# Out-projection, query and key/value projections moved between two key tiles of the scores

## The chip, the cores and the metric

The kernel runs on one core of one Trainium2 chip. A core has a matrix engine (TensorE, in the profile PE, its weight loads PEld) that writes to PSUM, and three engines that work on vectors: VectorE (DVE), ScalarE (ACT) and GpSimd (POOL). SyncE (SP) issues DMAs. Each engine works through its own queue in order; semaphores make one engine wait for another. The metric is the device time of one execution in microseconds (us). The kernel before takes 1353.22 us, the median of three runs.

## The reference

An input `x` (2048 x 256) goes through a cross attention over 1601 context rows of width 192 (and one learned key and value ahead of them, so 1602 keys), with 16 heads of width 64, and then through a feed-forward network with weights of +1 and -1.

```python
x1 = layernorm(layernorm_plain(x)) * g_norm
q, k, v = x1 @ Wq, ctx @ Wkv[:, :1024], ctx @ Wkv[:, 1024:]
k, v = [null_k; k], [null_v; v]            # 1602 keys
a = softmax(q k^T / 8, masked)             # per head
x = x + layernorm(concat(a v) @ Wout) * g_out
h = relu(s0 * [xn, -xn] @ k0) * 2;  h = relu(s1 * h @ k1) * 2
x = x + s2 * h @ k2                        # xn = layernorm(x); k0, k1, k2 are signs
```

The softmax needs the maximum of each query's scores before the exponentials, and the sum of the exponentials after them.

## The kernel before

The work is cut into units `(p, b)`: `p` counts eight pairs of heads, `b` four blocks of 512 queries, 32 units in all, `b` running fastest. The two heads of a pair lie in the two halves of the 128 partitions, so that a matmul of head 0 and one of head 1 use the two row halves of TensorE together. Keys are cut into 13 tiles of 128 (the last has 66).

One unit has three stages on PE.

*Scores* (loop over `k`, `exps` at line 284 and `max_chunk` at line 251). For each key tile, `sT` = keys times queries in full fp32 (L296). For tiles 0 and 1 the negated maxima `mT` are added by a small matmul with ones (L307), because key tiles are kept as differences to the tile two before (`keys_stepped`, line 216, on POOL), so that even and odd tiles accumulate in two PSUM buffers that are never restarted. ACT makes the exponential `e` (L309), and POOL adds all `e` up to `acc` (L498, L500). Beside this, in the same loop, PE computes the scores of the *next* unit a first time, with rounded operands, in 16 chunks (L259: four query tiles by four key ranges of 400), and DVE reduces each chunk to its maximum (L262). One chunk goes with each tile, two with tiles 0, 4 and 8 (`extra`). `max_combined` (L267) joins them to `mcol`.

*Values* (`weighted`, line 312): 13 pairs of matmuls accumulate `av`, with the two heads in the two column halves of the array (L316). After the third pair, `divided` (line 331) forms the denominators of the unit before (L334, `den`); DVE takes the reciprocal (L336, 3.36 us) and multiplies (L337) to `aoT`. ACT copies `av` to `avs` (L542).

*Projections*, with the full array: for the next pair of heads `project_v` (L230, copied by ACT at L238, and in the first block a row copied by DVE at L242) and `project_k` (L207; DVE writes `kT` at L211 and the rounded, filled `kr` at L212), spread over the blocks by `ahead`: block 0 takes values 0, 1 and keys 0; block 1 values 2, 3 and keys 1; block 2 keys 2, 3 and the differences on POOL (L221); block 3 nothing. Then `project_out` of the unit before (L324, added to `y_sb` by DVE at L329), `max_turned` (L272: `mcol` transposed by PE, spread by DVE to `mT` at L274), and `project_q` for the unit after the next (L196; ACT writes `qr` at L197 and `qT` at L198).

PSUM is used as two pairs of buffers of two banks each. `spare` holds the two `sT` buffers, then `av`, then some projections; `flex` holds the chunks of the maxima, `den`, the turned maxima and the other projections. A buffer is taken again only when what was in it has been read. The order is written out by hand (`manual_schedule`): each engine's queue has its instructions in the order in which the Python code issues them; only the waits are added. Weights are loaded by SP at the start of a pair's first unit for the pair after it (line 164), and run ahead as buffers come free.

Units 0 and 1 have something of their own: each normalizes one more input block of 512 rows (`input_root`, `input_normed`, on DVE and ACT), turned by PE in the projections (`input_turned`, L361). Units 28 and 29 prepare the first layer's weights `w0` on DVE (L526, L528), unit 30 normalizes the first output block. After the 32 units come the three layers of the feed-forward network.

## Time and profile before

| | us |
|---|---|
| median of 3 runs (1353.21 to 1353.57) | 1353.22 |
| the profiled execution | 1355.55 |
| its span, first to last instruction | 1353.7 |
| PE busy | 1329.3 |
| POOL busy | 994.8 |
| DVE busy | 880.7 |
| ACT busy | 607.7 |
| scores of a unit | 16.5 |
| values of a unit | 12.17 |
| projections, blocks 0, 1, 2, 3 | 8.68, 7.32, 6.44, 3.75 |

The stages are read from the starts of PE's matmuls in the middle of the run; they repeat from pair to pair within 0.1 us, so a pair of heads takes 4 x (16.5 + 12.17) + 26.2 = 141 us. The feed-forward network begins at about 1164 us.

How to read the profile: a group of instructions has its line, engine and operation, then `out<-in` by the program's names with shapes, a count, the busy time and mean length of one, and behind a bar the engine's idle time before them and what ended it. In a timeline, the columns are start, length, engine, line; neighbours of one group are merged (`x5`), and brackets give the idle time before and who ended it. [...] The granted PE clock was 0.992 of full on average.

### The profile page before, as it was taken

The page shows a single profiled execution, that of the slowest core. Times are in us where ns is not written, and L with a number is a line of the kernel's source. Part 1 is how long each engine was busy: PE and PEld are TensorE (multiplying, and loading weights), DVE is VectorE, ACT ScalarE, POOL GpSimd, SP SyncE. Part 2 cuts the span into 40 slices and gives each one's busy share as a digit, 9 for nine tenths or more (in the row PEclk, how much of TensorE's full clock was granted, in tenths as well). Part 3 has the DMA queues.
Part 4 walks back from the last instruction along what each step waited for, and adds up shares of the span by engine and source line. Part 5 has one row for each costly group of instructions (what it writes and reads, how often), then busy time and mean ns, then how long its engine had stood idle before and what let it go on. Part 6 is the DMA issues. An engine that isn't in the chain of part 4 may idle for free.

```text
span 1353.7 us, 16255 instructions
## 1 busy us (share of the span) xinstructions
PE 1329.3 (98%) x6528; PEld 664.6 (49%) x6528; DVE 880.7 (65%) x957; ACT 607.7 (45%) x655; POOL 994.8 (73%) x492
## 2 busy tenths in 40 slices
PE   6999999999999999999999999999999999999998
PEld 3544444444444444444444444444444443688887
DVE  5677776676667756686767656767676884464431
ACT  1666454445444454444544454454445557421220
POOL 4377987798888987798779877987798999711100
PEclk9799999999999999999999999999999999999999
DMA  5000000000000000000000000000000010000000
GB/s 136 4 1 7 0 1 8 8 1 0 8 1 7 1 1 8 7 1 1 7 8 1 1 8 8 0 1 5 0 16 1 1 39 0 1 0 16 16 16 16
DMA packets 14940, 12.31 MB, mean 9 GB/s; under 512 B 2240, under 2 KB 14784, under 8 KB 14864
## 3 DMA queue, kind: packets, MB, share of 16 engines
q1 hardware_dynamic: 13552, 9.70, 2.5%
q10 hardware_dynamic: 832, 1.23, 0.3%
q8 instruction: 51, 0.84, 0.3%
q0 software_dynamic: 480, 0.34, 0.1%
q14 instruction: 25, 0.20, 0.1%
HBM read 9.17 MB, written 2.10 MB: 8 GB/s over the span
## 4 chain that ended last, share of the span: by engine, by line
PE 93%; DVE 3%; ACT 2%; DMA 1%; issue 0%; POOL 0%; SPq 0%; ACTq 0%
PE sT L296 28%; PE av L316 27%; PE ps L592 10%; PE max L259 8%; PE psq L196 4%; PE po L324 4%; PE psv L230 3%; PE psk L207 3%; PE ps L615 2%; PE den L334 2%; ACT e L309 1%; PE sT L307 1%; DVE mx L262 1%; DMA x_sb<-in_x 1%; PE xT L361 0%
## 5 line engine op out<-in xcount | busy, mean ns | idle before, releaser
L500 POOL TENSOR_TENSOR acc<-acc,e 128x1024 f32<-128x1024 f32 (+1 forms) x352 | 847.3, 2407 | 27.6
L262 DVE TENSOR_REDUCE mx<-max 128x2 f32<-128x800 f32 (+1 forms) x512 | 481.3, 988 | 70.9 <-PE max L259 61.2
L309 ACT ACTIVATE e<-sT,maskb 128x1024 f32<-128x1024 f32 (+1 forms) x416 | 460.0, 1115 | 64.0 <-PE sT L296 38.0
L296 PE MATMUL sT<-qT,kT 64*128 64x512 f32 (+1 forms) x1664 | 444.4, 612 | 1.6 <-ACT e L309 1.4
L316 PE MATMUL av<-e,v 128*64 128x512 f32 (+1 forms) x1664 | 369.5, 594 | 1.0
L259 PE MATMUL max<-kr,qr 64*128 64x400 f32 (+1 forms) x1024 | 285.7, 568 | 2.3 <-DVE mx L262 1.5
L316 PEld LDWEIGHTS av<-e,v 128*64 128x64 f32 (+1 forms) x1664 | 116.7, 137 | 239.0 <-issue 219.3
L259 PEld LDWEIGHTS max<-kr,qr 64*128 64x128 f32 x1024 | 97.3, 186 | 187.2 <-DVE mx L262 149.7
L296 PEld LDWEIGHTS sT<-qT,kT 64*128 64x128 f32 (+1 forms) x1664 | 135.3, 181 | 104.8 <-ACT e L309 81.5
L498 POOL TENSOR_TENSOR acc<-e,e 128x1024 f32<-128x1024 f32 x32 | 75.5, 2358 | 147.6 <-ACT e L309 147.6
L542 ACT COPY avs<-av 128x512 f32<-128x512 f32 x32 | 18.8, 587 | 327.0 <-PE av L316 327.0
L336 DVE RECIPROCAL aoT<-den 128x512 f32<-128x512 f32 x31 | 104.1, 3357 | 70.0 <-PE den L334 70.0
L197 ACT ACTIVATE qr<-psq 128x512 fp32r<-128x512 f32 x32 | 19.1, 597 | 139.1 <-PE psq L196 139.1
L592 PE MATMUL ps<-h0hi,w 128*128 128x512 f32 x256 | 79.5, 392 | 0.0
L592 PE MATMUL ps<-h0lo,w 128*128 128x512 f32 x256 | 78.9, 389 | 0.0
L211 DVE TENSOR_TENSOR kT<-psk,keep 128x400 f32<-128x400 f32 (+1 forms) x32 | 18.4, 574 | 90.0 <-PE psk L207 89.8
L119 POOL TENSOR_TENSOR y_sb<-y_sb,gout_sb 128x256 f32<-128x256 f32 x12 | 9.3, 776 | 90.1 <-DVE y_sb L86 90.1
L581 DVE SCALAR_TENSOR_TENSOR h1lo<-ps,h1hi 128x1024 fp32r<-128x1024 f32 x16 | 19.6, 1224 | 69.0 <-ACT h1hi L580 69.0
L196 PE MATMUL psq<-xnT,wq 128*128 128x512 f32 x128 | 62.2, 610 | 0.6 <-DVE kT L211 0.6
L324 PE MATMUL po<-wo,aoT 128*128 128x256 f32 x256 | 61.5, 383 | 0.0
L329 DVE TENSOR_TENSOR y_sb<-po,y_sb 128x1024 f32<-128x1024 f32 x28 | 34.2, 1220 | 40.0 <-PE po L324 39.8
L580 ACT ACTIVATE h1hi<-ps 128x1024 fp32r<-128x1024 f32 x16 | 16.4, 1027 | 94.6 <-PE ps L592 94.6
(125 smaller groups left out, 1054.8 us busy)
## 6 DMA issues: line engine op xcount, KB each, us to landing
x_sb<-in_x SPq DMA_DIRECT2D x4, 512.0 KB, 8.7
out_x<-o SPq DMA_DIRECT2D x8, 256.0 KB, 2.1
wkv<-in_wkv SPq DMA_DIRECT2D x16, 96.0 KB, 2.1
wq<-in_wq SPq DMA_DIRECT2D x8, 128.0 KB, 2.3
wo<-in_wout SPq DMA_DIRECT2D x8, 128.0 KB, 2.1
xnT<-in_k SPq DMA_DIRECT2D x1, 1024.0 KB, 5.9
ctx_sb<-in_ctxT ACTq DMA_DIRECT2D x3, 300.0 KB, 7.9
xnT<-in_k SPq DMA_DIRECT2D x1, 512.0 KB, 3.9
```

The source lines that it names most:

```text
L196: nc.tensor.matmul(ps[:, 0, :], weights[p][0][:, c, :], xnT[:, b, c, :], start=c == 0, stop=c == 1)
L207: nc.tensor.matmul(ps[:, 0, :w], weights[p][1][:, c, 0, :], ctx_sb[:, c, keys], start=c == 0, stop=c == 1)
L259: nc.tensor.matmul(ps[:, j, :w], queries[p, b][1][rows, ts(t, 128)], pairs[p][2][rows, ds(start, w)], start=True, stop=True)
L262: nc.vector.tensor_reduce(maxima[p, b][:, t, :, c], ps[:, :, :w], AX.X, ALU.max)
L296: nc.tensor.matmul(ps[:n, j, :], kT[rows, ds(128 * k, n)], qT[rows, :], start=k < 2, stop=k >= 2, skip_group_check=k >= 2,)
L309: nc.scalar.activation(e[:n], ps[:n], AF.Exp, bias=maskb[:n, k : k + 1])
L316: nc.tensor.matmul(av[ts(j, DH), 0, :], v[:n, k, ts(j, DH)], e[:n, j, :], start=k == 0, stop=k == KC - 1)
L324: nc.tensor.matmul(pv[:, t, :], aoT[:, ts(t, 128)], weights[p][2], start=True, stop=True)
L336: nc.vector.reciprocal(aoT, ps)
L498: nc.gpsimd.tensor_tensor(acc, es[0], es[1], ALU.add)
L500: nc.gpsimd.tensor_tensor(acc[:m], acc[:m], es[k][:m], ALU.add)
L592: nc.tensor.matmul(ps[:, f, :], w(c)[:, ts(2 * g + f, 128)], parts[part][:, c, :], start=i == 0, stop=i == len(steps) - 1,)
```

## The change

The three stages become two and an insert. The function `projections(u)` holds what stood after the values; in all units but the first it is called inside the scores loop, ahead of tile 7 (`HALF`), so after tile 6 and its chunk. `project_out` there is that of the unit two back. `max_turned` now follows the values directly, and uses two matmuls against the identity, one for each 64 columns of `mcol`, in place of one transpose over the full array. All projections use `flex`. The doubled chunks go with tiles 0, 7 and 10. Unit 0 normalizes both remaining input blocks and calls `projections(0)` at its end. Buffers: `qT` three, `qr` two, `mx` one; `ones` becomes a view of `ones_r`. The work itself, operation by operation, is otherwise the same.

```diff
-    ones = cp.tile([128, DH], F32, name="ones")
+    ones_r = cp.tile([128, 128], F32R, name="ones_r")
+    ones = ones_r.bitcast(F32)[:, :DH]
...
-            qT = wp.tile([128, 512], F32, tag="qT", name=f"qT_{p}_{b}")
-            qr = wp.tile([128, 512], F32R, tag="qr", name=f"qr_{p}_{b}", bufs=1)
+            qT = wp.tile([128, 512], F32, tag="qT", name=f"qT_{p}_{b}", bufs=3)
+            qr = wp.tile([128, 512], F32R, tag="qr", name=f"qr_{p}_{b}")
...
-            nc.tensor.transpose(ps[:, 0, :128], mcol, ident)
+            for j in range(2):
+                nc.tensor.matmul(ps[ts(j, DH), 0, :128], mcol[:, ts(j, DH)], ident, start=True, stop=True)
...
-            po = spare(f"po_{p}_{b}")
+            po = flex(f"po_{p}_{b}")
...
-        extra = {0, 4, 8}
+        extra = {0, 7, 10}
+        HALF = 7
...
+        def projections(u):
+            nonlocal quotient
+            p, b = units[u]
+            if quotient is not None:
+                project_out(*quotient)
+                quotient = None
+            if u < 2:
+                input_turned(u + 2)
+            if u + 2 < len(units):
+                project_q(*units[u + 2])
+            if p + 1 < NP:
+                for n in ahead[b][0]:
+                    project_v(p + 1, n)
+                for n in ahead[b][1]:
+                    project_k(p + 1, n)
+                if b == 2:
+                    keys_stepped(p + 1)
...
+                    if k == HALF and u > 0:
+                        projections(u)
                     es.append(exps(p, b, k, sT))
...
-                if u < 2:
-                    input_normed(u + 2, *input_root(u + 2), beside=True)
+                if u == 0:
+                    roots = [input_root(c) for c in (2, 3)]
+                    for c in (2, 3):
+                        input_normed(c, *roots[c - 2], beside=True)
                     nc.scalar.activation(warm, eps_sb, AF.Exp)
...
-                    if k == 2 and last is not None:
-                        aoT = divided(*last, flex(f"den_{p}_{b}")[:, 0, :])
+                    if k == 2 and owed is not None:
+                        quotient = (*owed[:2], divided(*owed, flex(f"den_{p}_{b}")[:, 0, :]))
...
                 nc.scalar.copy(avs, av[:, 0, :])
-                if u < 2:
-                    input_turned(u + 2)
-                if p + 1 < NP:
-                    for n in ahead[b][0]:
-                        project_v(p + 1, n, spare if n % 2 else flex)
-                    for n in ahead[b][1]:
-                        project_k(p + 1, n, spare if n % 2 else flex)
-                    if b == 2:
-                        keys_stepped(p + 1)
+                owed = (p, b, avs, acc)
+                if nxt is not None:
+                    max_turned(*nxt)
+                if u == 0:
+                    projections(0)
                 if nxt is None:
                     uT = turned(0)
-                if last is not None:
-                    project_out(*last[:2], aoT)
-                if nxt is not None:
-                    max_turned(*nxt)
-                if u + 2 < len(units):
-                    project_q(*units[u + 2])
-                last = (p, b, avs, acc)
+                    project_out(*quotient)
+        last = owed
```

More of the change, by code (lines that the diff above doesn't have):

```diff
@@ L156, in xattn_ffn @@
         maskb = ap.tile([128, KC], F32, name="maskb")
-        ones_r = ap.tile([128, 128], F32R, name="ones_r")
         mcol = ap.tile([128, 128], F32, name="mcol")
@@ L253, in max_chunk @@
             if n == 0:
-                maxima[p, b] = wp.tile([128, 4, 2, 4], F32, tag="mx", name=f"mx_{p}_{b}")
+                maxima[p, b] = wp.tile([128, 4, 2, 4], F32, tag="mx", name=f"mx_{p}_{b}", bufs=1)
             start, w = CHUNKS[c]
@@ L413, in xattn_ffn @@
         nc.gpsimd.memset(maskb, 0.0)
-        nc.gpsimd.memset(ones, 1.0)
         nc.gpsimd.memset(fan, 1.0)
@@ L460, in xattn_ffn @@
         begin.__exit__(None, None, None)
-        last = None
+        owed = None
+        quotient = None
[4 more added lines that the diff above has]
+                project_out(*quotient)
+                quotient = None
+            if u < 2:
[9 more added lines that the diff above has]
+                    keys_stepped(p + 1)
         with tc.manual_schedule():
```

## The prediction

> **What bounds the kernel now.** I read the page first: engines, then the chain. TensorE (PE) is busy nearly always and the chain is 93% PE, so one must see which part of its time is work and which is waiting with a matmul open.

> ```profile
> span 1353.7 us, 16255 instructions
> PE 1329.3 (98%) x6528; PEld 664.6 (49%) x6528; DVE 880.7 (65%) x957; ACT 607.7 (45%) x655; POOL 994.8 (73%) x492
> PE 93%; DVE 3%; ACT 2%; DMA 1%; issue 0%; POOL 0%; SPq 0%; ACTq 0%
> ```

> Then the busy time by window: scores, attention times values, projections of unit (3,1), then the next scores.

> ```profile
> 511.10:527.59 16.49, 16.45 (x89) 7.18 (x88) 14.14 (x16) 14.44 (x15) 11.96 (x6) 1.00 0.01 4
> 527.59:539.76 12.17, 12.17 (x56) 3.93 (x56) 5.23 (x4) 1.00 (x1) 11.86 (x5) 1.00 0.01 2
> 539.76:547.08 7.32, 7.32 (x39) 5.23 (x37) 3.37 (x4) 1.33 (x3) 4.97 (x3) 1.00 0.00 0
> ```

> Columns: length, then PE, weight loads, DVE, ACT, POOL. In the scores three engines are over 85% busy; afterwards DVE, ACT and, in the projections, POOL have time. The timeline of the next scores shows what paces them.

> ```profile
> 552.44 2.22 ACT L309 ACTIVATE e<-sT,maskb 128x1024 f32<-128x1024 f32 x2 [0.19 <-PE sT L296]
> 555.03 2.21 ACT L309 ACTIVATE e<-sT,maskb 128x1024 f32<-128x1024 f32 x2 [0.37 <-PE sT L296]
> 552.56 4.79 DVE L262 TENSOR_REDUCE mx<-max 128x2 f32<-128x804 f32 x5 [0.20 <-PE max L259]
> 557.54 4.79 DVE L262 TENSOR_REDUCE mx<-max 128x2 f32<-128x800 f32 x5 [0.20 <-PE max L259]
> ```

> Four tiles and five chunks take 4.98 us: five reduces of 4.79 and one gap. PE waits for both engines:

> ```profile
> PEld max L259 <- DVE mx L262: 145.3, 336, 0.7
> PEld sT L296 <- ACT e L309: 71.0, 184, 0.5
> ```

> PE's own streams are shorter. From starts in the timeline: a score tile 0.855 (two passes of 0.43), a shift 0.215, a chunk 0.175. Then 13 x 0.855 + 2 x 0.215 + 16 x 0.175 = 14.35 of 16.5: about 2.1 us per unit is round trips through two-buffer PSUM. Values (14 pairs of 0.86) and projections run dense.

> The last view is DVE's short operations and POOL's in the projections:

> ```profile
> L212 DVE SCALAR_TENSOR_TENSOR kr<-drop,nullk,kT x32: 635/698/2126, 14.4 to 1002.3; 128x400 fp32r<-128x400 uint8 x24, 128x402 fp32r<-128x402 uint8 x8
> 578.87 0.56 DVE L211 TENSOR_TENSOR kT<-psk,keep 128x400 f32<-128x400 f32 x1
> 579.47 2.12 DVE L212 SCALAR_TENSOR_TENSOR kr<-drop,nullk,kT 128x400 fp32r<-128x400 uint8 x1
> ```

> ```profile
> 573.73 7.43 POOL L500 TENSOR_TENSOR acc<-acc,e 128x1024 f32<-128x1024 f32 x3
> 581.67 1.94 POOL L221 TENSOR_TENSOR kT<-kT 128x66 f32<-128x66 f32 x3 [0.51 <-DVE kr L212]
> ```

> `kr` costs 0.64 us, or up to 2.1: the long one at 579.47 ends 0.43 after POOL's addition ends (581.16), and so do the other long ones. Today PE works on and nobody waits.

> [...]`kr`, with two SBUF inputs, waits for POOL's end; the reduces, the eviction of `psk` (0.56 to 0.58) and `mT`, with one operand in PSUM, never vary. [...]from the last stream of `psq` (ends 511.00) to the first of `sT` (511.20) it is 0.2 us. [...]

> **The change, part by part.** Per-unit accounting, T0 = end of the last `av` stream. Latencies from the timeline: a result is there 0.165 after its stream, DVE starts 0.045 later, ACT 0.115; PE's next stream starts 0.16 after an engine's end; reduces follow at 0.90.

> *Mode switches.* Before: rows, columns, full, rows: three. After: rows, full, rows, columns, rows: four. +0.2 per unit. The maxima in halves stay in `av`'s mode: two passes of 128 columns, 0.21 against 0.11, +0.1. Sum +0.3. `mT` (0.68) starts at T0+0.42, done at 1.10; the first tile streams from 0.41 to 1.27, so it hides `mT`.

> *First half, tiles 0 to 6.* The same waits as today: tile 6 streams at 8.0, chunk 7 at 8.86 to 9.04. `po` needs chunk 6's buffer: chunk 6 streams at 7.72, reduced at 9.09; `po` at 9.25, just the mode switch. Nothing gained or lost.

> *Projections.* Streams as before: `po` 1.72, `psq` 1.71, `psv` 1.83 each, `psk` 1.34. All use the two `flex` buffers now, so two waits appear. b=1: `psk` waits until ACT has copied `psv2`: 0.57. b=2: the second `psk` waits for both copies of `psq`: 0.28.

> *Second half, tiles 7 to 12.* It has eight chunks in six tiles, 8 x 0.90 = 7.2 us of DVE against 6 x 0.855 + 8 x 0.175 = 6.5 of PE: it is DVE's pace that sets it. Without obstacles reduce 8 starts 1.4 after the last projection, and chunk 10 streams at +2.57. The end of the last projection to the next `av` is then 7.9. Check on b=3: 9.25 + 3.43 (`po`, `psq`) + 7.9 = 20.6, against 16.5 + 3.75 = 20.25 now: +0.3, just the switch and the halves, and the 2.1 us of round trips stay. ACT's copies of `psq` and `psv` (0.6 each) stand ahead of tile 7's exponential; they are done before tile 7 has streamed, save in b=3, where chunk 9 waits 0.4 for the second copy of `psq`; DVE's slower pace covers that. But reduce 8 is queued on DVE behind the evictions of `psk`, and POOL, which adds from T0+4.4 in steps of 2.43 (ends 14.0, 16.45, 18.9), is now always busy there:
> - b=3: no `psk`. +0.3.
> - b=0: last stream ends 17.68, `kT` until 18.46, `kr` waits for 18.9, ends 19.4, column copy, reduce 8 ends 20.4, chunk 10 at 20.6 instead of 20.25. The row copy (L242) waits for 16.45, ahead of `kT`. 0.3 + 0.3 = +0.6.
> - b=1: ends 16.88, `kT` until 17.66, `kr` 19.3, reduce 8 ends 20.3, chunk 10 at 20.43 instead of 19.45: 1.0. With 0.57 and 0.3, less 0.1 that overlaps: +1.8.
> - b=2: first `kr` at 14.8 ends 16.9; `kT` 17.4; POOL's next, lengthened, ends 19.1, second `kr` 19.5; reduce 8 ends 20.5, chunk 10 at 20.64 instead of 18.21: 2.4. With 0.28 and 0.3, less 0.1: +2.9.

> One pair: 5.6 us. Six ordinary pairs: 33.6. Bounds: [...]with later waits absorbed, 0.3 + 0.8 + 0.5 + 0.3 = 1.9; with POOL half a step off against me, 8.5.

> *Moved and added elsewhere.* POOL's key differences (3.9 us, L221) stand between additions 6 and 7; POOL needs 30 us of 35, its lag ends inside the next unit, nobody waits. SP's loads of weights are issued a pair ahead, `wo` lands 2.1 us after issue: no wait. `project_out` two back reads an `aoT` long finished; if it weren't, `po` would stop PE, but L337 ends at least 2 us before T0, and `po` comes 9 us later. `ones` as a view of `ones_r` takes one POOL memset from the start, off the path.

> *First pair.* Unit 0 normalizes both remaining input blocks before `avs`: ACT at present starts its eight operations at 72.47 and needs 3.9; the second statistics (2.2 on DVE), eight more (3.9) and the table load end at about 83.7, against `av`'s end at 78.9. `avs`, `xnT`, then `psq` wait: +4.6. Unit 1: no `po` yet (-1.7), `psq` waits for `xnT` (+1.2), plus its 1.8: +1.3. Units 2, 3: 3.2. Sum 9.1.

> *Last pair.* 3 x 0.3; `w0` (3.4 and 4.4 us, ends 1100.9 against T0 = 1098.7) now stands ahead of `mT` with no projections to hide it: +0.8 and +2.0; in the last unit `po` costs about 0.8, the rest under the last exponentials. Sum 4.5.

> Total 33.6 + 9.1 + 4.5 = 47 on the profiled span 1353.7 (its execution 1355.55, 1.85 outside the span). The median is 1353.22; the difference is laid on it: 1400.

> **Rivals.** (1) [...]`kr` finds gaps. Then 6 x 1.9 + 7.5 + 4.5 = 23, 1376. For: it takes 0.64 in all b=0 units today; against: there POOL had finished, here it is in mid-chain. (2) Faster: the break lets ACT finish tiles 5 and 6 and DVE two chunks under the projections, so tiles 7 and 8 need not wait, and half of the 2.1 us of round trips goes: 1.0 - 0.3 = 0.7 per unit, 27 units, 19; less the 9 at the two ends: 1343. For: the idle DVE and ACT in the third window; against: only two chunks fit into PSUM, and eight follow in six tiles. It decides if reduce 8 follows its matmul within 0.4 us on average. (3) Moved work without effect: only if gains of rival 2 meet losses of mine. That the program doesn't do as told is excluded: its instruction order shows `po`, `psq`, `psv`, `psk` after chunk 7 and tile 7 after them.

> **How the numbers follow.** Forecast (1375 to 1422) 0.72; rival 1 (1366 to 1380) 0.13; rival 2 0.12; within 0.2%, about what a measurement can tell from no change, 0.03. The range is 1366 to 1420: it leaves out rivals 2 and 3 and a little of the upper bound. Slower 0.85.

> **What would show it.** Right: scores before tile 7 about 9.2 from T0, b=2 longest against before (38 us per unit), `kr` at 1.5 to 2.1 inside the scores and the reduce after it late, a PE gap of over 4 us after unit 0's values. Wrong: `kr` at 0.64, or a second half under 7 us.

## The result and the profile after

The kernel after takes 1401.94 us (median of 4 runs, 1399.09 to 1403.38), the kernel before 1353.22 (1352.55 to 1353.57) on the same chip: 1.0358 times as long, 95% interval 1.034 to 1.0376. The profiled execution took 1401.85 us with a span of 1400.1, 46.4 more than before's 1353.7.

The page of the kernel after, in the lines that answer to those of before (engines' busy time, then the chain by engine):

```profile
span 1400.1 us, 16434 instructions
PE 1339.9 (96%) x6624; PEld 676.1 (48%) x6624; DVE 896.3 (64%) x957; ACT 604.5 (43%) x652; POOL 987.2 (71%) x491
...
PE 81%; DVE 12%; ACT 4%; POOL 1%; issue 1%; DMA 1%; ACTq 0%; SPq 0%; DVEq 0%; POOLq 0%
```

PE's busy time rose by 11, the span by 46: the kernel doesn't work much more, it waits. The chain's share of DVE went from 3% to 12%. That tells the engine; the stages tell the place. Busy time by window in unit (3,2): the turned maxima (`mt`) with the first half of the scores, projections, second half, values; then the second half of unit (3,0). The columns are length, PE, weight loads, DVE, ACT, POOL, granted clock.

```profile
569.90:579.10 9.20, 9.20 (x54) 4.14 (x50) 7.36 (x8) 7.28 (x8) 4.69 (x2) 1.00 0.00 0
579.10:585.55 6.45, 6.45 (x24) 3.64 (x22) 3.52 (x4) 2.19 (x3) 6.21 (x4) 1.00 0.00 0
585.55:595.73 10.18, 7.67 (x41) 3.32 (x41) 10.14 (x10) 5.55 (x6) 9.19 (x9) 1.00 0.00 0
595.73:607.80 12.07, 12.07 (x56) 4.07 (x58) 5.73 (x5) 0.98 (x1) 11.68 (x6) 1.00 0.01 1
...
512.12:520.15 8.03, 7.42 (x41) 3.40 (x40) 7.78 (x10) 5.50 (x5) 6.55 (x4) 1.00 0.01 2
```

Only the third window is bad: of 10.18 us PE has 7.67, DVE is busy in 10.14. DVE's timeline there, with POOL's two lines between:

```profile
584.21 0.57 DVE L211 TENSOR_TENSOR kT<-psk,keep 128x400 f32<-128x400 f32 x1 [1.84 <-PE psk L207]
584.82 2.03 DVE L212 SCALAR_TENSOR_TENSOR kr<-drop,nullk,kT 128x400 fp32r<-128x400 uint8 x1
586.77 0.56 DVE L211 TENSOR_TENSOR kT<-psk,keep 128x400 f32<-128x400 f32 x1
587.37 2.12 DVE L212 SCALAR_TENSOR_TENSOR kr<-drop,nullk,kT 128x400 fp32r<-128x400 uint8 x1
589.41 7.30 DVE L262 TENSOR_REDUCE mx<-max 128x2 f32<-128x804 f32 x8
...
581.63 7.42 POOL L525 TENSOR_TENSOR acc<-acc,e 128x1024 f32<-128x1024 f32 x3
589.57 4.35 POOL L221 TENSOR_TENSOR kT<-kT 128x66 f32<-128x66 f32 x6 [0.52 <-DVE kr L212]
```

POOL's third addition ends at 589.05, the second `kr` at 589.49, 0.44 later; only then does DVE begin the eight reductions, 3.9 us after the second half began. The first of them, that of chunk 8, is called reduction 8 below. Over the whole run the group of `kr` (least, median, longest in ns; the median was 698 before):

```profile
L212 DVE SCALAR_TENSOR_TENSOR kr<-drop,nullk,kT x32: 635/1739/2127, 14.5 to 1027.1; 128x400 fp32r<-128x400 uint8 x24, 128x402 fp32r<-128x402 uint8 x8
```

From the starts of PE's matmuls (in the timeline their lengths overlap: those of `av` are 0.59 us long and start in pairs 0.43 us apart), the stages of every ordinary pair after, against the unit's sum before (in pairs 5 and 6, counted from 0, block 1 has halves of 9.14 and 8.45 with the same sum):

| block | `mt` | first half | projections | second half | values | sum | before | more |
|---|---|---|---|---|---|---|---|---|
| 0 | 0.32 | 8.89 | 8.57 | 8.03 | 12.07 | 37.88 | 37.35 | +0.5 |
| 1 | 0.32 | 8.89 | 7.71 | 8.71 | 12.07 | 37.70 | 35.99 | +1.7 |
| 2 | 0.32 | 8.89 | 6.43 | 10.20 or 11.55 | 12.07 | 37.9 or 39.3 | 35.16 | +2.8 or +4.1 |
| 3 | 0.32 | 8.89 | 3.64 | 7.68 | 12.07 | 32.60 | 32.42 | +0.2 |

The 46.4 us: six ordinary pairs +35.0 (5.83 each), the first pair +12.3, the last with the feed-forward network +2.6, and -3.5 in the opening. The opening's part is hardly the change's: the values of unit 0 end at 75.1 to 79.3 us over the twelve kernels of this study (78.9 in before, 75.4 in after, 76.7 in experiment 4, whose opening is that of after, and 75.1 in before with experiment 8's edit), and PE's granted clock in the first 50 us is 0.80 in before and 0.86 in after (0.90 in the first 51 us of experiment 9).

The first pair's part begins in unit 0. PE and ACT there, in the timeline:

```profile
75.73 1.09 PE L363 MATMUL xT<-ident,y_sb 128*128 128x128 f32 x8
81.67 3.78 PE L196 MATMUL psq<-xnT,wq 128*128 128x512 f32 x4 [4.85 <-ACT xnT L364]
85.24 5.00 PE L230 MATMUL psv<-wkv,ctx_sb 96*128 96x128 f32 x32
...
79.06 1.28 ACT L542 ACT_TABLE_LOAD   x1
80.46 0.57 ACT L569 COPY avs<-av 128x512 f32<-128x512 f32 x1
80.93 0.69 ACT L364 ACTIVATE xnT<-xT,gn_sb 128x512 f32<-128x512 f32 x1
```

PE stands for 4.85 us, and afterwards is slower: 3.78 and 5.00 where experiment 9 below has 1.98 and 3.74. The granted clock is 0.74 from 84.0 to 91.5 us.

### The profile page after: what moved, and what is told of

It reads as the page before. It is cut to its first block, busy times and chain, and to the rows that moved or that the text cites. A ratio compares the mean times of both kernels' runs of the same rounds, so it can differ in the third digit from the quotient of the medians.

```text
span 1400.1 us, 16434 instructions
## 1 busy us (share of the span) xinstructions
PE 1339.9 (96%) x6624; PEld 676.1 (48%) x6624; DVE 896.3 (64%) x957; ACT 604.5 (43%) x652; POOL 987.2 (71%) x491
## 4 chain that ended last, share of the span: by engine, by line
PE 81%; DVE 12%; ACT 4%; POOL 1%; issue 1%; DMA 1%; ACTq 0%; SPq 0%; DVEq 0%; POOLq 0%
PE av L318 25%; PE sT L298 22%; PE ps L609 9%; PE max L259 6%; DVE mx L262 5%; PE po L326 4%; PE psq L196 4%; DVE kr L212 3%; PE psv L230 3%; ACT e L311 2%; PE psk L207 2%; PE ps L632 2%; PE den L336 2%; DVE kT L211 1%; PE sT L309 1%; POOL acc L525 1%
## 5 line engine op out<-in xcount | busy, mean ns | idle before, releaser
L525 POOL TENSOR_TENSOR acc<-acc,e 128x1024 f32<-128x1024 f32 (+1 forms) x352 | 840.3, 2387 | 37.9 <-ACT e L311 11.9
L262 DVE TENSOR_REDUCE mx<-max 128x2 f32<-128x800 f32 (+1 forms) x512 | 480.3, 986 | 72.6 <-PE max L259 63.8
L298 PE MATMUL sT<-qT,kT 64*128 64x512 f32 (+1 forms) x1664 | 451.0, 620 | 1.7 <-ACT e L311 1.4
L259 PE MATMUL max<-kr,qr 64*128 64x400 f32 (+1 forms) x1024 | 288.4, 578 | 31.6 <-DVE mx L262 26.7
L523 POOL TENSOR_TENSOR acc<-e,e 128x1024 f32<-128x1024 f32 x32 | 75.4, 2358 | 191.4 <-ACT e L311 191.4
L259 PEld LDWEIGHTS max<-kr,qr 64*128 64x128 f32 x1024 | 98.2, 188 | 206.6 <-DVE mx L262 152.6
L298 PEld LDWEIGHTS sT<-qT,kT 64*128 64x128 f32 (+1 forms) x1664 | 139.3, 184 | 96.6 <-ACT e L311 66.2
L276 DVE TENSOR_TENSOR mT<-mt,fan 128x512 fp32r<-128x512 f32 x32 | 22.1, 690 | 98.4 <-PE mt L274 98.4
L609 PE MATMUL ps<-h0lo,w 128*128 128x512 f32 x256 | 78.9, 389 | 0.0
L339 DVE TENSOR_TENSOR aoT<-avs,aoT 128x512 f32<-128x512 f32 x32 | 59.6, 1863 | 2.6
L207 PE MATMUL psk<-ctx_sb,wkv 96*128 96x400 f32 (+1 forms) x128 | 51.2, 532 | 7.6 <-DMA ctx_sb<-in_ctxT 4.8
```

Of the source, the lines that this page charges most:

```text
L207: nc.tensor.matmul(ps[:, 0, :w], weights[p][1][:, c, 0, :], ctx_sb[:, c, keys], start=c == 0, stop=c == 1)
L259: nc.tensor.matmul(ps[:, j, :w], queries[p, b][1][rows, ts(t, 128)], pairs[p][2][rows, ds(start, w)], start=True, stop=True)
L262: nc.vector.tensor_reduce(maxima[p, b][:, t, :, c], ps[:, :, :w], AX.X, ALU.max)
L298: nc.tensor.matmul(ps[:n, j, :], kT[rows, ds(128 * k, n)], qT[rows, :], start=k < 2, stop=k >= 2, skip_group_check=k >= 2,)
L523: nc.gpsimd.tensor_tensor(acc, es[0], es[1], ALU.add)
L525: nc.gpsimd.tensor_tensor(acc[:m], acc[:m], es[k][:m], ALU.add)
```

## The experiments

Theory: `kr`, which reads two operands from SBUF, waits for POOL's additions (every long one in the traces of before and after ends 0.43 to 0.44 us after one), and in the new place reduction 8, and so PE, is queued behind it. Rivals: the break with its mode switches costs by itself (A); any work ahead of reduction 8 costs, however short (B); the wait for two flex buffers instead of four (C, D). A fourth question is the first pair. All times are medians beside the kernel before on the same chip (1352.66 for the first four, 1354.95 for the next four, 1354.22 for the last two).

**Experiment 1: `kr` without the second SBUF operand.**

```diff
-nc.vector.scalar_tensor_tensor(kr[:, keys], drop[:, keys], nullk[:, 0:1], kT[:, keys], ALU.mult, ALU.add)
+nc.vector.scalar_tensor_tensor(kr[:, keys], drop[:, keys], nullk[:, 0:1], ps[:, 0, :w], ALU.mult, ALU.add)
```

> The kernel after, but kr (L212) adds drop*nullk to psk in PSUM instead of to kT in SBUF, so that it has one SBUF operand; it leaves out the masking of the keys for the maxima only. Theory ([...]reduce 8 is queued behind it): kr 0.60 to 0.75 us in all 32, second half of the scores in b=2 down from 10.2 or 11.55 to about 8.3, b=1 from 8.7 to about 7.8, b=0 from 8.0 to about 7.8; per pair 3.4 to 4.6 less, 24 to 32 in all: 1370 to 1378, point 1374. Rival A (the break itself, its mode switches, costs the time): 1398 to 1403. Rival B (any work between the projections and reduce 8 costs, however short[...]): kr short but the second halves within 0.3 of those of after, 1392 or more.

1372.1 us (1370.4 to 1374.61), 1.0147 times before (1.0132 to 1.0162): by the ratios about 29 of the 48 us are gone. The group, and DVE in a unit of block 2:

```profile
L212 DVE SCALAR_TENSOR_TENSOR kr<-drop,nullk,psk x32: 617/623/625, 14.7 to 1001.4; 128x400 fp32r<-128x400 uint8 x24, 128x402 fp32r<-128x402 uint8 x8
...
573.38 0.57 DVE L211 TENSOR_TENSOR kT<-psk,keep 128x400 f32<-128x400 f32 x1 [0.33 <-PE psk L207]
573.87 0.62 DVE L212 SCALAR_TENSOR_TENSOR kr<-drop,nullk,psk 128x400 fp32r<-128x400 uint8 x1
574.62 3.69 DVE L262 TENSOR_REDUCE mx<-max 128x2 f32<-128x804 f32 x4
```

The same operation with one operand in PSUM took 617 to 625 ns in all 32, beside the same additions of POOL. All second halves become 7.68 to 8.03; the granted clock, which fell in four of the block 2 units of after, is 0.992 on average here and 0.987 there. The order of the work was not touched, so A, as the main cause, and B for blocks 1 and 2 fall: work of ordinary length stands ahead of reduction 8 at no cost there.

**Experiment 2: key projections first**, so that `kT` and `kr` stand on DVE ahead of `po`, `psq` and `psv`.

```diff
+            if p + 1 < NP:
+                for n in ahead[b][1]:
+                    project_k(p + 1, n)
+                if b == 2:
+                    keys_stepped(p + 1)
             if quotient is not None:
...
-                for n in ahead[b][1]:
-                    project_k(p + 1, n)
-                if b == 2:
-                    keys_stepped(p + 1)
```

> The kernel after, with the key projections (and POOL's key differences) put first among the projections, so that kT and kr stand on DVE a few us ahead of reduce 8; nothing else moves. Theory: kr stays at 1.5 to 2.1 us in b=1 and 2, but the second halves come to 7.6 to 7.9 in all four units; b=2 gets a new wait of 0.5 before its third projection, since the second kT is queued behind the first long kr; b=1 loses the wait of psk for psv2. Per pair 3.3 to 4.8 less: 1367 to 1378, point 1372. Rival A (break and mode switches): 1398 to 1403. Rival C (the wait for flex buffers in the projections is the main part): the projection stages keep their length and the time stays above 1390.

1367.82 us (1367.58 to 1371.75), 1.0123 (1.0106 to 1.014). The second halves are 7.68 to 7.72 in all blocks, the projection stages 8.56, 7.21, 6.33 and 3.64: b=1's wait for `psv2` was 0.50 us, b=2's 0.10. C had the smallest part. One thing came out otherwise: `kr`, now a few us earlier, is mostly short here (median 639 ns). For blocks 0 and 1 this run therefore does not separate place from length. For block 2 it does: the second `kr` is still 1.94 long in every pair, yet the second half is 7.68, and reduction 8 waits for its chunk and not for DVE:

```profile
564.14 1.94 DVE L212 SCALAR_TENSOR_TENSOR kr<-drop,nullk,kT 128x400 fp32r<-128x400 uint8 x1
566.00 1.21 DVE L331 TENSOR_TENSOR y_sb<-po,y_sb 128x1024 f32<-128x1024 f32 x1
568.22 7.52 DVE L262 TENSOR_REDUCE mx<-max 128x2 f32<-128x804 f32 x8 [1.01 <-PE max L259]
```

In two units of block 1 a `kr` of 2.80 did cost time, to what stood behind it in the new place:

```profile
810.15 2.80 DVE L212 SCALAR_TENSOR_TENSOR kr<-drop,nullk,kT 128x400 fp32r<-128x400 uint8 x1
812.88 1.21 DVE L331 TENSOR_TENSOR y_sb<-po,y_sb 128x1024 f32<-128x1024 f32 x1
```

The eviction of `po` came late, its flex buffer with it, and the projections of these two units took 8.67 instead of 7.21.

**Experiment 3: block 3 normalized by DVE**, to free ACT in unit 0.

```diff
-input_normed(c, *roots[c - 2], beside=True)
+input_normed(c, *roots[c - 2], beside=c == 2)
```

> The kernel after, with the normalization of input block 3 in unit 0 done by DVE (four operations, as the opening does for block 0) instead of by ACT's eight; both square roots stay where they are. Theory for the first pair (avs waits in ACT's queue behind sixteen operations and a table load, PE idles 4.85 us and runs slower for a while after): ACT reaches avs before av ends, the gap after unit 0's values is under 1.5 us and psq and psv take their usual 1.7 and 1.8: 5 to 7.5 less, 1394.5 to 1397, point 1395.5. Rival (the gap is the two statistics on DVE or the table load, not the eight operations): under 1.5 us gained, 1400 to 1402.

1403.76 us (1401.39 to 1405.49), 1.0379 (1.0363 to 1.0394): nothing gained, a miss. Here is DVE, then ACT:

```profile
74.90 9.75 DVE L87 TENSOR_SCALAR y_sb<-x_sb,mv_x,rstd_x 128x256 f32<-128x256 f32 x4
...
85.48 0.68 DVE L276 TENSOR_TENSOR mT<-mt,fan 128x512 fp32r<-128x512 f32 x1
...
80.11 0.57 ACT L569 COPY avs<-av 128x512 f32<-128x512 f32 x1
80.57 0.69 ACT L364 ACTIVATE xnT<-xT,gn_sb 128x512 f32<-128x512 f32 x1
```

Each of the four operations took about 2.45 us, one step of POOL's additions (2.43), and `mT` and DVE's half of `xnT` stood behind them. They have one tensor from SBUF, where `kr` has two. The same operation from 1236 us on in after took up to 0.90 us instead of 0.41 when it met an operation of POOL, and ended 0.15 after it. So the edit moved the work into another wait for POOL, and says nothing of ACT's part.

**Experiment 4: the block of projections between the last tile and the values** instead of between tiles 6 and 7.

```diff
-                    if k == HALF and u > 0:
-                        projections(u)
...
+                if u > 0:
+                    projections(u)
                 if nxt is not None:
                     max_combined(*nxt)
```

> The kernel after, with the block of projections put between the last score tile and the values instead of between tiles 6 and 7 (unit 0 as in after). Maxima in halves, buffers and the order within the block are unchanged; what is no longer there is the break inside the scores, one mode switch, and DVE's reductions queued behind kT and kr. Theory: seven pairs lose nearly all of their 5.8 extra, but for the halves (0.1 per unit), up to 0.85 per pair of flex waits, and a short wait of po for the reduction of chunk 14; first pair's unit 0 still costs its 7.5: 1360 to 1372, point 1365. Rival A (the mode switches): 0.2 per unit less than after, about 1395. Rival D (the two flex buffers instead of four are the cost): above 1385.

1377.18 us (1376.79 to 1377.55), 1.0183 (1.0168 to 1.0198): 25 less than after by the medians, 24 by the ratios, and 5 more than the upper end expected. A and D, as expectations of 1395 and above 1385, fall. It is also the cleanest look at a long `kr` that costs nothing, in a unit of block 2:

```profile
580.37 1.44 DVE L212 SCALAR_TENSOR_TENSOR kr<-drop,nullk,kT 128x400 fp32r<-128x400 uint8 x1
581.74 0.56 DVE L211 TENSOR_TENSOR kT<-psk,keep 128x400 f32<-128x400 f32 x1
582.33 2.13 DVE L212 SCALAR_TENSOR_TENSOR kr<-drop,nullk,kT 128x400 fp32r<-128x400 uint8 x1
...
581.09 2.79 PE L318 MATMUL av<-e,v 128*64 128x512 f32 x12
```

`av` runs on beside them. This is before's situation. What remains is 0.42 to 0.47 per unit (0.93 in b=1, with the wait for `psv2`): 0.21 for `mt`, and 0.31 at the end of the scores, where `po` waits for the reduction of chunk 14 and its flex buffer, while before `av` goes on in `spare`.

**Experiment 5: normalization in one ACT operation** (scale and bias together), eight operations instead of sixteen in unit 0. A flag, not shown below, keeps the old form for the other callers.

```diff
-nc.vector.tensor_scalar(nm, mv[:, :, 0], -1.0, None, ALU.mult)
+nc.vector.scalar_tensor_tensor(nm, mv[:, :, 0], -1.0, r, ALU.mult, ALU.mult)
...
-nc.scalar.activation(dst[:, t, :], src[:, t, :], AF.Identity, bias=nm[:, j : j + 1])
-nc.scalar.mul(dst[:, t, :], dst[:, t, :], r[:, j : j + 1])
+nc.scalar.activation(dst[:, t, :], src[:, t, :], AF.Identity, bias=nm[:, j : j + 1], scale=r[:, j : j + 1])
```

> The kernel after, with the normalization of input blocks 2 and 3 in unit 0 in one ACT operation per 128 rows (scale 1/std, bias -mean/std) instead of two: ACT does 8 operations of 0.5 us there instead of 16; DVE does no more than in after. Theory for the first pair (avs and xnT wait in ACT's queue behind the sixteen operations and the table load): ACT is free about 4 us earlier, at the end of av; PE's gap after unit 0's values falls from 4.85 to under 1.2 us, and psq and psv after it come back to about 1.7 and 1.8: 5 to 7.5 less, 1394 to 1397, point 1395. Rival ([...]halving its work only makes it wait): under 1.5 us gained, 1400 to 1403.

1398.24 us (1395.65 to 1400.55), 1.0323 (1.0298 to 1.0348): 3.7 less than after by the medians, 4.7 by the ratios, where 5 to 7.5 were expected. Unit 0's projection stage fell from 15.8 to 12.2 (8.6 in before). ACT's eight operations need 4.2 us, but the second four wait for DVE:

```profile
75.38 2.32 DVE L139 SCALAR_TENSOR_TENSOR nm<-mv_x,rstd_x 128x4 f32<-128x4 f32 x1
77.74 2.08 ACT L145 ACTIVATE y_sb<-x_sb,nm,rstd_x 128x256 f32<-128x256 f32 x4 [0.37 <-DVE nm L139]
77.82 2.34 DVE L570 TENSOR_SCALAR sgn<-sgn 128x2 f32<-128x2 f32 x1
80.64 1.94 DVE L573 TENSOR_TENSOR s_out<-s_out,s_sb 128x1 f32<-128x1 f32 x1
```

Operations on a handful of elements take 2.3 us, `mT` stands behind them on DVE, and PE waits 2.63 us for it: theory and rival (that DVE's small operations, which wait for POOL, hold ACT up) were both half right.

**Experiment 6: experiments 2 and 5 together.**

> Key projections first and normalization in one operation, together. Theory: the two causes are separate, but key projections first already fill part of PE's gap in unit 0 (its projection stage was 11.4 instead of 15.8, against 8.6 in later units), so that 2.5 to 4 us remain to be gained over key projections first alone: 1363 to 1366, point 1364. What stays above before is 0.15 to 0.2 per unit (mode switch and halves) and the last pair. Rival (the remaining cost is spread over all units): 1367 to 1369.

1366.56 us (1363.8 to 1367.57), 1.0086 (1.0067 to 1.0106), against 1.0123 for experiment 2: 0.4% less, though the two intervals meet and the median lies above the range expected. The size fits, but not the cause. Between the two traces the first pair became 1.4 longer, not 2.5 to 4 shorter; the six ordinary pairs became 3.5 shorter, because the two long units of block 1 did not occur (all of block 1 has 7.21 here). Unit 0's projection stage was 12.7, against 11.4 in experiment 2, because `mT` again stood behind the sign preparation on DVE (`s_out`, L574 there, 1.94 us) and PE behind `mT`:

```profile
79.96 0.68 DVE L282 TENSOR_TENSOR mT<-mt,fan 128x512 fp32r<-128x512 f32 x1
80.78 1.06 PE L369 MATMUL xT<-ident,y_sb 128*128 128x128 f32 x8 [2.10 <-DVE mT L282]
82.62 3.68 PE L202 MATMUL psq<-xnT,wq 128*128 128x512 f32 x4 [0.78 <-ACT xnT L370]
```

**Experiment 7: nine chunks ahead of the break, seven behind**, on top of experiment 6.

```diff
-        extra = {0, 7, 10}
+        extra = {0, 3, 10}
```

> As key projections first and normalization in one operation, with the extra chunks of the maxima at tiles 0, 3 and 10 instead of 0, 7 and 10: nine chunks in seven tiles ahead of the break and seven in six behind it, instead of eight and eight. Theory (behind the break DVE's eight reductions pace, 7.68; ahead of it the tile's own round trip of 1.2 us paces and DVE has room for a ninth): second half 7.0 to 7.3, first half 8.9 to 9.2; 0.2 to 0.5 less per unit, 1350 to 1358, point 1354. Rival (the halves are paced by the tiles' round trips in both, or the ninth chunk costs ahead of the break what it saves behind): within 0.1 per unit of the kernel with eight and eight, 1361 to 1366.

1398.22 us (1397.23 to 1398.3), 1.0324 (1.0304 to 1.0344), a clear miss. The halves are 9.19 and 7.39 (7.78 in block 2) where experiment 6 has 8.89 and 7.68: +0.30 and -0.29, so the rival was right on them. And the projections took 10.15, 8.6, 7.5 and 3.64. DVE's timeline in block 0, then PE's:

```profile
358.05 2.67 DVE L218 SCALAR_TENSOR_TENSOR kr<-drop,nullk,kT 128x402 fp32r<-128x402 uint8 x1
360.82 1.21 DVE L337 TENSOR_TENSOR y_sb<-po,y_sb 128x1024 f32<-128x1024 f32 x1
...
362.09 3.84 PE L236 MATMUL psv<-wkv,ctx_sb 96*128 96x128 f32 x32 [1.32 <-DVE y_sb L337]
```

The shift of 0.3 us against POOL's additions was enough for `kr` to meet one most of the time (median 2676 ns, longest 2766), with the eviction of `po` behind it. The cost of `kr`'s wait came back at another consumer.

**Experiment 8: the kernel before with experiment 1's edit**, to see whether `kr`'s wait costs anything where no reduction of the scores stands behind it.

> The kernel before, with kr added from psk in PSUM instead of from kT in SBUF, as a control (it leaves out the masking of the keys for the maxima only). Theory[...]: kr short in all 32, time within 1 us of before, 1352 to 1354. Rival (the long kr also costs in before, through flex buffers or POOL's key differences): 2 to 6 us less, 1347 to 1351.

1353.3 us (1351.4 to 1356.08), 0.9995 (0.9985 to 1.0005), with `kr` at 617 to 624 in all 32. The long `kr` cost next to nothing in before: in two units the scores take 16.72 and 16.80, and 16.5 with this edit.

**Experiment 9: everything together**: experiments 1, 2 and 5, and the sign preparation moved from unit 0 to unit 7.

```diff
+                if u == 7:
+                    nc.vector.tensor_scalar(sgn, s_sb[:, 0:2], 0.0, None, ALU.is_ge)
...
                 av = spare(f"av_{p}_{b}")
...
-                if u == 0:
-                    nc.vector.tensor_scalar(sgn, s_sb[:, 0:2], 0.0, None, ALU.is_ge)
```

> Everything at once: kr from PSUM, key projections first, normalization in one ACT operation, and the five small operations that prepare the weights' signs (L563 to L567) moved from unit 0's values to unit 7's, since in the kernel with key projections first and one operation they held mT, and behind it PE, for 2.1 us (it leaves out the masking of the keys for the maxima only). Theory: PE's 2.1 us wait ahead of unit 0's xT goes, psq and psv after it run at 1.7 and 1.8 again; the odd b=1 units with 1.7 us more, where the eviction of po waits on DVE behind a long kr, go too. What stays over before is 0.18 per unit, 5.5 us, and 2 to 3 at the two ends: 1357 to 1362, ratio to before 1.003 to 1.007. Rival (the break still hides round trips once nothing is queued ahead of reduction 8, so that all of it together beats before): under 1352. Rival (the first pair's loss is from another cause): no less than 1363.

1364.13 us (1361.17 to 1364.74), 1.0077 (1.0064 to 1.0091), 2 over the range expected, where the time alone would suit the second rival (1363 or more). The stages speak against that rival. PE in unit 0:

```profile
77.77 1.04 PE L369 MATMUL xT<-ident,y_sb 128*128 128x128 f32 x8
79.59 1.98 PE L202 MATMUL psq<-xnT,wq 128*128 128x512 f32 x4 [0.78 <-ACT xnT L370]
81.41 3.74 PE L236 MATMUL psv<-wkv,ctx_sb 96*128 96x128 f32 x32
```

The stage is 8.76 long, in before 8.60 with `mt`, and the first pair takes 113.2 against 113.0: with ACT's queue shortened and DVE's small operations away, unit 0's loss is gone. Six ordinary pairs take 5.9 more than in before. Of this 1.0 is the moved sign preparation: in unit 7 three of its five operations take 2.0 to 2.2 us, and `mT` comes late for the next unit, whose first half is 9.92 instead of 8.89. Yet the whole does not beat before, and 1.0 us would not change that: the rival that the break, once free, brings a gain falls.

**Experiment 10: experiment 9 with nine and seven chunks.**

> The same with extra chunks at tiles 0, 3 and 10 (nine chunks ahead of the break, seven behind). In the earlier kernel with this split the projections took 1.6, 1.4, 1.1 and 0 us more in b=0 to 3. Theory (that was kr at 2.3 to 2.8 us again, with the eviction of po queued behind it and so a flex buffer for the next projection): with kr short the projections take 8.6, 7.2, 6.3 and 3.6 as in the kernel with eight and eight, the halves 9.2 and 7.4, and the time is that of the kernel beside it within 1.5 us. Rival (the ninth chunk itself delays the projections, through its reduction): the projections stay over 0.5 longer, 15 us or more above the kernel beside it.

1363.09 us (1360.28 to 1364.31), 1.0064 (1.0049 to 1.008), the same as experiment 9 within the intervals. The projections are 8.57, 7.21, 6.46 and 3.64 again with the halves at 9.19 and 7.39. So what experiment 7 lost, 32 us against experiment 6, was the long `kr` and what stood behind it. No version of the kernel after beat before.

## Why the prediction was right, step by step

*Direction and size.* 1400 was predicted, 1401.94 measured; the range and the sign held. The mechanism is the one named: `kr` waits for POOL's addition, with reduction 8 behind it (experiment 1 takes the wait away in the same order of work, and 29 us go; experiment 8 shows that the wait alone is nearly harmless; "nobody waits" in the prediction was half a us off in the whole run). The last `kr` was forecast to end 19.4, 19.3 and 19.5 us after T0 in blocks 0, 1 and 2; in pair 3 it ends after 19.39, 19.38 and 19.59.

*Ordinary pairs.* Predicted +0.6, +1.8, +2.9, +0.3 for blocks 0 to 3, measured +0.5, +1.7, +2.8 or +4.1, +0.2. A pair 5.6 against 5.83; six pairs 33.6 against 35.0.

- Mode switch and halves: +0.3 predicted, about +0.18 measured. In block 3, which has no keys, it is +0.21 for `mt`, +0.07 for the two halves of the scores together (16.57 against 16.50) and -0.10 for the values. So the halves of the maxima cost 0.2 where 0.1 was put, and the added switch almost nothing where 0.2 was put, the author's estimate from the 0.2 us between `psq` and `sT` in before (511.00 to 511.20); the sum is oversized by 0.1 us per unit.
- First half: 9.25 from T0 to `po` predicted, 0.32 + 8.89 = 9.21 measured.
- Flex waits: 0.57 for b=1 (0.50 by experiment 2), 0.28 for b=2 (0.10).
- The second half without obstacles: 7.9 predicted, 7.68 measured. Rival 2 (half of the round trips hidden) falls with 16.57: the break gives at most a tenth or two back. (Its sum had put the two ends at 9, where the forecast itself has 9.1 + 4.5.)
- Without `kr`'s wait for POOL a pair was put at +1.9. Experiment 1's second pair takes 142.56 against 140.95, +1.6.
- Left out: the longer block 2. In four of seven of these units the second half takes 11.55 instead of 10.20, after the same waits. The windows from the second `kr` on, a unit of each kind:

```profile
440.00:449.70 9.70, 7.90 (x36) 3.57 (x36) 8.28 (x8) 4.95 (x6) 8.71 (x9) 0.82 0.00 0
587.00:595.70 8.70, 6.37 (x34) 2.83 (x34) 8.66 (x9) 5.30 (x6) 7.79 (x8) 1.00 0.00 0
```

The granted clock fell to 0.82 in the first; a score tile there took 1.91 instead of 1.02. It is 1.35 us each time, three times in the six pairs: 4 us, a term that the prediction does not have, which covers what the oversized mode switches left. That 33.6 and 35.0 lie so close is in part luck. Narrower windows show which units are hit:

```profile
439.47:442.88 3.41, 1.31 (x6) 0.48 (x6) 3.37 (x3) 2.10 (x2) 2.82 (x3) 1.00 0.00 0
442.88:446.30 3.42, 3.26 (x10) 1.82 (x12) 2.38 (x4) 0.74 (x1) 3.11 (x5) 0.50 0.00 0
586.24:589.65 3.41, 1.93 (x11) 0.52 (x8) 3.37 (x4) 1.95 (x2) 2.81 (x3) 1.00 0.00 0
589.65:593.06 3.41, 2.53 (x14) 1.22 (x14) 3.41 (x5) 1.46 (x3) 3.10 (x5) 1.00 0.00 0
```

The clock halves for just 3.41 us, from 442.88. All its changes in this trace lie whole multiples of 3.413 us apart: between those at 43.52, 81.07, 149.34 and 442.88 us, for instance, there are 37.55, 68.27 and 293.54 us, 11, 20 and 86 times that length. In the slow units nearly all of PE's waiting falls into one such window (busy 1.31 of 3.41 us); in the others it is split over two (1.93 and 2.53), and the clock stays. The program is the same in all pairs, and the slow ones are those where the waits fall on this grid so that one window has 1.31 us of PE: pairs 0, 2, 4 and 6, where the clock is 0.50 from 149.34, 442.88, 736.43 and 1029.98 us. In pairs 1, 3 and 5 the windows have 1.88 to 1.93, and the clock stays.

*First pair.* 9.1 predicted, 12.3 measured. Unit 0: +4.6 predicted, +7.5 measured. The gap itself was right (4.85 against usually under 1 us); the term that was missing is PE's slower clock after it (0.50 from 81.07 to 87.90), 2.9 us: from the start of `psq` to the end of `psv` it is 8.4, in experiment 9, without the gap, 5.5. Units 1 to 3: 4.5 predicted, 4.8 measured, from two misses that cancel: +0.6 instead of +1.3 in unit 1, +4.3 instead of +3.2 in units 2 and 3 (unit 2 is one of those that lose clock, 0.50 from 149.34 to 152.75). ACT's lateness against the end of `av` was put at 4.8 (83.7 against 78.9) and came out at 4.9 (80.35 against 75.41).

*Last pair.* 4.5 predicted, 2.6 measured. Of `w0`'s effect on `mT`, 0.8 and 2.0 predicted, the first did not show (unit 29's first half 8.89) and the second was 0.65 (unit 30: 9.55 instead of 8.89). DVE's operation ahead of `w0`, the multiplication to `aoT`, took 1.57 and 1.59 us instead of 2.88 in before, so `w0` began 3.4 us before the end of the values instead of 2.2, and its first operation was done when `mt` came.

*Opening.* Nothing predicted, -3.5 measured; see above. Without it the sum would be 50 instead of 46.4, against 47 predicted: the closeness of the spans is luck in part, since the underrated first pair, the overrated last one and the opening nearly cancel.

What stays open: what moves the length of the opening from run to run, and why the timed runs of experiment 9 lie some 3 us above its profiled one.

## What to carry to other kernels

When work is moved, list for each engine what is then queued behind every moved operation, and give each a length under the traffic of its new place, not the one it has where it is now: an operation of 0.64 us that waits for another engine's additions was 2.1 us there, and cost 4.3 us in each pair of heads of 141 (six pairs, after against experiment 1). An operand in PSUM instead of SBUF took the coupling away (617 to 625 ns in all 32, experiment 1) for one changed word, though here that word also leaves out a mask, so that the operand would have to be prepared for it; moving the operation changed where it met the other engine and what stood behind it. Before a break in a paced loop is expected to give relief, check that its buffers can hold more than the loop already does: here they could not, and 16.5 us stayed 16.6.
